# One product and one scan for two states: PSUM banks handed out in pairs, in a two-layer scan and expert network

## The chip, the cores and the metric

The kernel runs on one core of one Trainium2 chip. The metric is the device time of one execution in microseconds (us): 3631.21 us, the median of three runs of the kernel before (3628.26 to 3633.24).

## The reference, cut to what matters

The input is `x`, 8 images of 256 channels and 32x32 positions. Two layers follow each other, and each adds a mixer and then a feed-forward part to its input. Layer 0 mixes with a selective scan over the 1024 positions of an image, for 512 channels with 16 states each, and then sends each token to the two best of 8 experts. Layer 1 has depthwise convolutions, a smaller scan (64 channels, 16 states), and a feed-forward part for the 511 best-ranked tokens of an image. The part that the change touches is the scan, the same in both layers:

```
dt  = softplus(dtr @ W_dt + b_dt);  A = -exp(A_log)
dA  = exp(dt[..., None] * A)                         # per channel and state
dBu = (dt * xs)[..., None] * Bm[:, :, None, :]
h[t] = dA[t] * h[t-1] + dBu[t],  h[-1] = 0
y[t] = sum over states of h[t] * Cm[t];   y = y + xs * Dp;   y = y * silu(z)
```

## The kernel before, in words

Positions are cut into halves of N = 512. A *unit* is one half of one image; there are 16, in the order image 0 first half, image 0 second half, image 1 first half and so on. In a unit the 512 channels are four chunks of 128 partitions, taken two at a time (`cp`), and the 16 states are taken two at a time (`sp`). So a unit has 2x8x2 = 32 calls of `scan_pair`, each for one chunk and two states. Layer 1's scan (`mamba_scan`) has four groups of two images and 16 calls in each, so that there are 576 calls and 1152 states in all.

One call of `scan_pair` does the following. POOL multiplies `dtx` by the broadcast rows of B for both states at once into `dbu` (L801). Then, for each of the two states: ACT writes exp(dt*A) into a PSUM bank `h` (L806); DVE scans in place (L809), from zero in a first half and from the saved state in a second half; in a first half ACT copies the last column into `state` (L813); DVE multiplies by the row of C into `dbu` (L814). In some calls (`PAIRED`) POOL adds the two halves of `dbu` (L818). Then PE sums into `y`, in layer 0 by transposes (L793) and in layer 1 by a matmul with the identity (L828). At the end of each `cp`, DVE multiplies `y` by the gate (L875).

PSUM has eight banks of 128x512 floats. Two hold `y`. The other six are one list that two pools share: `da`, the scan states, up to three at a time, and `mm`, all other matmul outputs, up to four (five late in the program).

A planner sets the order. Every piece of work is a `step` with an engine, a cost in us, a priority (a due time), and the buffers that it reads, writes or fills. `Flow.run` takes the steps one after the other by estimated start time and emits the instructions in that order; each engine then runs its own list strictly in order, with semaphores between engines. `UNIT_AT` and `PLAN` hold the due times of units and of the later stages, and the costs in the `step` calls are figures written by hand. `warm` puts filler matmuls on `still` (L534, L538) where the planner sees PE idle. SP issues nearly all DMAs; POOL issues the indirect ones: `put` (L1129) into the experts' and tokens' slots, and gathers `ys` (L1316, L1704).

Other steps that are named below: `norm`, which POOL ends by adding a column to `xn` (L670); `delta`, which makes `dt` and `dtx` (L761 to L773); `start_turned`, in which POOL scales `xs` by the column D in two instructions (L849); `tokens`, where ACT evicts a PSUM bank (L950) and DVE takes eight more columns of the same bank (L957); the convolution taps of layer 1 on DVE (L1407); and `finish`, which ends in the last transfer.

Of the kernel before, what the change touches and what calls it, by code (L numbers as in the profile page):

```python
# [12 lines left out]
ALU = mybir.AluOpType  # L13
# [24 lines left out]
PAIRED = [3, 3, 2, 2, 0, 0, 7, 4, 4, 6, 1, 4, 0, 1, 4, 4, 4, 8, 7, 0]  # L38
# [3 lines left out]
UNIT_AT = [17, 48, 78, 109, 147, 178, 208, 241, 273, 304, 335, 368, 400, 432, 484, 518]  # L42
PLAN = [
    dict(put=7.28, experts=(179.64, 6.48), combine=(394.29, 2.87), taps=(475.51, 4.65), mamba=463.45, assemble=(516.15, 0.19), ranks=379.03, ffn=(527.6, 8.1), finish=(603.63, 3.02)),
    dict(put=10.63, experts=(348.85, 7.5), combine=(472.91, 4.35), taps=(597.89, 4.49), mamba=562.12, assemble=(556.68, 3.79), ranks=589.82, ffn=(817.97, 2.22), finish=(801.17, 11.23)),
    dict(put=5.04, experts=(457.79, 5.2), combine=(519.92, 3.42), taps=(600.24, 6.32), mamba=640.73, assemble=(726.06, 11.14), ranks=770.31, ffn=(920.6, 1.57), finish=(976.7, 8.85)),
    dict(put=5.12, experts=(583.29, 4.39), combine=(599.78, 2.06), taps=(821.99, 1.8), mamba=843.01, assemble=(797.83, 6.56), ranks=923.56, ffn=(978.1, 0.54), finish=(1005.56, 4.79)),
]

WARM = True  # L50

# [30 lines left out]
AHEAD = 100  # L82
# [33 lines left out]
class Pool:  # L116
# [4 lines left out]
    def __init__(self, make, n, in_order=True, free=None, late=None):  # L121
        self.make, self.free, self.in_order = make, [(0.0, i) for i in range(n)] if free is None else free, in_order
        self.bufs, self.queue, self.taken, self.out, self.most, self.late = [], [], 0, 0, n, late or (float("inf"), n)
        self.heir, self.got, self.handed = None, {}, 0

    def has(self, n, buf):
# [3 lines left out]
        return len(self.free) >= n and self.out + n <= most and buf.turn < self.taken + n  # L130
# [8 lines left out]
    def back(self, at, slot):  # L139

        self.out -= 1
        if self.heir is None or self.handed < len(self.bufs):
            self.free.append((at, slot))
            return
# [11 lines left out]
    def take(self, buf):  # L156
        slot = min(self.free)
        self.free.remove(slot)
# [18 lines left out]
class Flow:  # L177
# [32 lines left out]
    def run(self):  # L210
# [17 lines left out]
        def earliest(s):  # L228
# [4 lines left out]
            for b in s.fresh:  # L233
                if b.v is None:
# [3 lines left out]
                    at = max(at, sorted(b.pool.free)[k - 1][0] + HOP)  # L238
# [4 lines left out]
        def choose(e, limit):  # L243

            heap, seen, able = ready[e], [], []
            while heap and len(seen) < 40 and heap[0][0] <= limit:
# [3 lines left out]
                if at is not None:  # L250
                    switch = s.table is not None and s.table != tables[0]
                    able.append((s.prio + (4 if switch else 0), s.n, s, at, s.us + (SWITCH if switch else 0.0)))
# [3 lines left out]
            for i in able:  # L256

                if i is able[0] and i[3] <= now[e] + 0.05 or i[3] + i[4] <= able[0][3] + 0.3:
                    return i[2:]
            return able[0][2:] if able else None  # L260

        while left:
            while scans and scans[0][2].waits < 0:
                heapq.heappop(scans)
            limit = scans[0][0] + AHEAD if scans else float("inf")
# [36 lines left out]
def layers(g, ctx, x, a, out):  # L302
# [17 lines left out]
    def setup_ps():  # L320
        return g.t(g.psum, [P, N], "mm0", bufs=1)

# [33 lines left out]
    nc.vector.tensor_scalar_mul(neg_a, neg_a, -1.0)  # L356
# [90 lines left out]
    def x_tile(i):  # L447
# [3 lines left out]
    free = [(0.0, i) for i in range(6)]  # L451

# [4 lines left out]
        "mm": tiles("mm", [P, N], 4, where=g.psum, in_order=False, free=free, late=(LATE, 5)),  # L457
        "da": tiles("mm", [P, N], 3, where=g.psum, free=free),
# [87 lines left out]
    def other_weights(prio):  # L546
# [35 lines left out]
        def rest():  # L582
# [13 lines left out]
            nc.vector.tensor_scalar_mul(neg_a1, neg_a1, -1.0)  # L596
            nc.vector.tensor_scalar_mul(skip1, g.ident, ch1[:, COL_D : COL_D + 1])

        step(PE, 5.0, prio + 1, products, [loaded, w_out_t, w_xm], [t])
# [32 lines left out]
    def norm(i, prio):  # L632
# [35 lines left out]
        def shifted():  # L668
            for k in range(KC):
                nc.gpsimd.tensor_scalar(xn.v[:, k, :N], xn.v[:, k, :N], lnw[:, k, 1:2], None, ALU.add)  # L670

        gpsimd(1.2, prio + 2.2, shifted, [], [xn])

    def project(i, cp, z, prio):
# [30 lines left out]
        for n in range(2):  # L705
# [10 lines left out]
            step(ACT, 0.6, prio + n + 0.2, lambda t=t, pre=pre: nc.scalar.copy(pre.v[:, 3:], t.v), [t], fills=[pre])  # L716
# [37 lines left out]
    def delta(parts, dts, dtxs, xs, prio, soon=False):  # L754

        v, l = banks(2), buf("sq")
        for n in range(2):
            left, right, made = parts[n]
            step(PE, 0.9, prio, lambda n=n, left=left, right=right: nc.tensor.matmul(
# [13 lines left out]
        gpsimd(2.4, prio + 2, lambda: nc.gpsimd.tensor_tensor(dtxs.v, dts.v, xs.v, ALU.mult), [dts, xs], [dtxs])  # L773

    def dt_of(i, cp, prio):
# [6 lines left out]
        delta(parts, dts, dtxs, u[f"xs{cp}"], prio, soon=i == 0)  # L782
# [15 lines left out]
    def scan_pair(prio, dts, dtxs, n, bt, ct, y, scales, initial, last, stop, paired, turned=False):  # L798

        dbu = buf("dbu")  # L800
        gpsimd(2.45, prio, lambda: nc.gpsimd.tensor_tensor(  # L801
            dbu.v, dtxs.v[:, n : n + 1].to_broadcast(wide2), bt.v, ALU.mult), [dtxs, bt], [dbu], scan=True)
        for j in range(2):

            h = buf("da")
            step(ACT, 0.69, prio, lambda j=j, h=h: nc.scalar.activation(  # L806
                h.v, dts.v[:, n], AF.Exp, scale=scales(j)), [dts], [h], table="exp", scan=True)
            at = [] if initial is None else [initial[0]]
            step(DVE, 1.25, prio, lambda j=j, h=h: nc.vector.tensor_tensor_scan(  # L809
                h.v, h.v, dbu.v[:, j], 0.0 if initial is None else initial[1](j), ALU.mult, ALU.add),  # L810
                [dbu, *at], [h], scan=True)
            if last is not None:
                step(ACT, 0.19, prio, lambda j=j, h=h: nc.scalar.copy(last[1](j), h.v[:, N - 1 :]), [h], fills=[last[0]])  # L813
# [1109 lines left out]
```

## Time and profile before

| | |
|---|---|
| median of three runs | 3631.21 us |
| profiled execution: its time, its span | 3627.38 us, 3625.7 us |
| granted TensorE clock, mean | 0.936 |
| DVE, ACT, POOL busy | 2813.1, 2248.5, 2407.9 us |
| PE busy, of which filler L534 | 3075.2, 354.5 us |
| scans: first start, last start | 58.4, 3412.8 us |
| last product of a unit by its gate; end of the span | 2683, 3626 us |

The page of a profile gives busy time by engine first, and then groups of instructions: line, engine, operation, the buffers written and read, the shapes, how many; after the first bar the busy time in us and the mean of one in ns; after the second bar how long the engine had stood idle just before instructions of the group, and what ended most of that. The view of waits sums the same idle time by the instruction that waited and the one that released it: total us, times, longest. The view of stretches gives for each window its length and each engine's busy time with the number of instructions, then the granted clock, the share of the DMA engines and GB/s. In the timeline a row is its start, its length, engine, line, operation. A buffer of a scan state appears in the profile as `mm`.

### The profile page before, as it was taken

The page shows a single profiled execution, that of the slowest core. Times are in us where ns is not written, and L with a number is a line of the kernel's source. Part 1 is how long each engine was busy: PE and PEld are TensorE (multiplying, and loading weights), DVE is VectorE, ACT ScalarE, POOL GpSimd, SP SyncE. Part 2 cuts the span into 40 slices and gives each one's busy share as a digit, 9 for nine tenths or more (in the row PEclk, how much of TensorE's full clock was granted, in tenths as well). Part 3 has the DMA queues.
Part 4 walks back from the last instruction along what each step waited for, and adds up shares of the span by engine and source line. Part 5 has one row for each costly group of instructions (what it writes and reads, how often), then busy time and mean ns, then how long its engine had stood idle before and what let it go on. Part 6 is the DMA issues. An engine that isn't in the chain of part 4 may idle for free. (4 is left out here: it accounts for less than half of the span.)

```text
span 3625.7 us, 43571 instructions
## 1 busy us (share of the span) xinstructions
PE 3075.2 (85%) x13495; PEld 2061.2 (57%) x13495; DVE 2813.1 (78%) x3924; ACT 2248.5 (62%) x4241; POOL 2407.9 (66%) x1716
## 2 busy tenths in 40 slices
PE   8777878789988878978988899988888888898968
PEld 4444454545756555645655566565566665675546
DVE  4889789889877986987787989767788748858841
ACT  4466465456767656856876676766586656746533
POOL 4787678578777867996786786655686842645431
PEclk9998999899998998989999989999899988999989
DMA  6343333345745535545554568565577776886845
GB/s 234 128 132 125 119 128 127 114 139 169 247 133 191 180 133 171 184 153 177 184 184 151 169 198 267 195 201 187 171 225 254 247 243 210 296 272 218 281 150 181
DMA packets 276325, 677.00 MB, mean 187 GB/s; under 512 B 31015, under 2 KB 114861, under 8 KB 276094
## 3 DMA queue, kind: packets, MB, share of 16 engines
q1 hardware_dynamic: 257662, 623.87, 52.1%
q0 software_dynamic: 18432, 50.36, 4.4%
q8 instruction: 108, 1.77, 0.2%
q14 instruction: 123, 1.01, 0.1%
HBM read 572.92 MB, written 101.19 MB: 186 GB/s over the span
## 5 line engine op out<-in xcount | busy, mean ns | idle before, releaser
L801 POOL TENSOR_TENSOR dbu<-dtx,bc 128x1024 f32<-128x1024 f32 x556 | 1310.8, 2373 | 299.0 <-DMA bc<-rows 109.0
L809 DVE TENSOR_TENSOR_SCAN mm<-mm,dbu 128x512 f32<-128x512 f32 x570 | 697.3, 1223 | 252.5 <-ACT mm L806 195.1
L806 ACT ACTIVATE mm<-dt,neg_a 128x512 f32<-128x512 f32 x1152 | 766.6, 688 | 102.0 <-DVE dbu L814 93.8
L814 DVE TENSOR_TENSOR dbu<-mm,bc 128x512 f32<-128x512 f32 x1108 | 765.8, 691 | 50.7 <-PE y L828 0.4
L809 DVE TENSOR_TENSOR_SCAN mm<-mm,state,dbu 128x512 f32<-128x512 f32 x568 | 728.5, 1283 | 58.2 <-ACT mm L806 35.6
L793 PE MATMUL y<-ident,dbu 128*128 128x128 f32 x3628 | 533.8, 288 | 257.5 <-POOL dbu L818 122.5
L793 PEld LDWEIGHTS y<-ident,dbu 128*128 128x128 f32 x3628 | 433.4, 147 | 428.1 <-POOL dbu L818 163.1
L813 ACT COPY state<-mm 128x1 f32<-128x1 f32 x576 | 91.4, 161 | 613.8 <-DVE dbu L814 588.2
L1240 PE MATMUL mm<-we,hid 128*128 128x256 f32 x1632 | 409.4, 405 | 36.6 <-ACT hid L1224 28.9
L818 POOL TENSOR_TENSOR dbu<-dbu 128x512 f32<-128x512 f32 x214 | 278.8, 1304 | 208.2 <-DVE dbu L814 196.7
L1240 PEld LDWEIGHTS mm<-we,hid 128*128 128x128 f32 x1632 | 322.7, 203 | 118.3 <-ACT hid L1224 42.9
L1218 PE MATMUL mm<-xbt,we 128*128 128x256 f32 x1536 | 368.2, 391 | 13.5 <-ACT xbt L1206 3.5
L534 PE MATMUL y<-still 128*128 128x512 bf16 x1329 | 354.5, 406 | 0.0
L1218 PEld LDWEIGHTS mm<-xbt,we 128*128 128x128 f32 x1536 | 295.4, 196 | 79.1 <-issue 12.9
L728 PE MATMUL mm<-pre,w_tap 128*128 128x512 f32 (+3 forms) x512 | 244.2, 620 | 11.4 <-ACT pre L716 9.5
L534 PEld LDWEIGHTS <-still 128*128 128x128 bf16 x1329 | 135.8, 103 | 148.8 <-issue 51.3
L436 ACT ACT_TABLE_LOAD x169 | 216.8, 1283 | 3.0
L1704 POOL DMA_INDIRECT ys<-y,slot_t x64 | 65.4, 1021 | 214.6 <-DVE xc L1714 107.3
L1316 POOL DMA_INDIRECT ys<-slots_y,slot x128 | 128.8, 1007 | 114.1 <-DVE xo L1337 32.1
L728 PEld LDWEIGHTS mm<-pre,w_tap 128*128 128x128 f32 x512 | 95.7, 196 | 133.1 <-issue 99.9
L1224 ACT ACTIVATE hid<-mm,we 128x256 f32<-128x256 f32 x384 | 151.6, 475 | 29.1 <-PE mm L1218 25.8
L711 PE MATMUL mm<-xn,w_pre 128*128 128x512 f32 x256 | 134.5, 649 | 23.1 <-POOL xn L670 21.1
(287 smaller groups left out, 4651.2 us busy)
## 6 DMA issues: line engine op xcount, KB each, us to landing
bc<-rows SPq DMA_DIRECT2D x608, 512.0 KB
we<-in_W SPq DMA_DIRECT2D x80, 514.0 KB
we<-in_W SPq DMA_DIRECT2D x80, 512.0 KB
xb<-slots_x SPq DMA_DIRECT2D x92, 256.0 KB
slots_y<-xo SPq DMA_DIRECT2D x92, 256.0 KB
xc<-x SPq DMA_DIRECT2D x64, 256.0 KB
we<-in_W12f SPq DMA_DIRECT2D x22, 512.0 KB
slots_x<-xg SPq DMA_DIRECT2D x10, 1024.0 KB
```

What stands on the lines that cost most here:

```text
L436: nc.scalar.preload_act_table_set(tables[name])
L534: nc.tensor.matmul(live[0].v[:, 0], still, wide, start=False, stop=False)
L728: nc.tensor.matmul(tc_.v[:, cut:], w_tap[:, c, j], pre.v[:, cut + j : j + N], start=j == 3, stop=j == 0)
L793: nc.tensor.matmul(y.v[:, n, k * P : (k + 1) * P], src[:, k * P : (k + 1) * P], g.ident, start=start and k == 0, stop=stop and k == N // P ...
L801: gpsimd(2.45, prio, lambda: nc.gpsimd.tensor_tensor(dbu.v, dtxs.v[:, n : n + 1].to_broadcast(wide2), bt.v, ALU.mult), [dtxs, bt], [dbu], ...
L806: step(ACT, 0.69, prio, lambda j=j, h=h: nc.scalar.activation(h.v, dts.v[:, n], AF.Exp, scale=scales(j)), [dts], [h], table="exp", scan=True)
L809: step(DVE, 1.25, prio, lambda j=j, h=h: nc.vector.tensor_tensor_scan(h.v, h.v, dbu.v[:, j], 0.0 if initial is None else initial[1](j), AL ...
L814: step(DVE, 0.68, prio, lambda j=j, h=h: nc.vector.tensor_tensor(dbu.v[:, j], h.v, ct.v[:, j], ALU.mult), [h, ct], [dbu], scan=True)
L818: gpsimd(1.3, prio + 2.3, lambda: nc.gpsimd.tensor_tensor(dbu.v[:, 0], dbu.v[:, 0], dbu.v[:, 1], ALU.add), [], [dbu])
L1218: nc.tensor.matmul(tv[:, f], we[0].v[:, at : at + P], xbt.v[:, k], start=k == 0, stop=k == KC - 1)
L1224: nc.scalar.activation(hid.v[:, f], tv[:, f % 2], func, bias=we[0].v[:, at : at + 1])
L1240: nc.tensor.matmul(to, hid.v[:, f, h * P : (h + 1) * P], we[1].v[:, f * C : (f + 1) * C], start=extra is None and f == 0, stop=f == FC - 1,)
```

## The change

1. *Two states in two banks.* The six banks are allocated as three tiles of two. The pool `da` now hands out whole pairs (at most two), and `mm` hands out single halves, first those whose neighbour is taken. In `scan_pair` both exponentials go into one pair. In a first half one scan runs over all 1024 columns, and in both halves one product does both states, as does one copy of the last columns.
2. *From zero in the middle.* For the one scan to start anew at column 512, the decay there has to be zero. `delta` sets the first column of `dt` to 1e30 after `dtx` is made, and A is kept at or below -1e-27, so that the exponential is zero.
3. *Readers of one bank.* The state copy is made to follow the product, with a priority one later, and `raw` to follow ACT's eviction.
4. *POOL.* The shift at the end of `norm` and the scaling in `start_turned` become tensor_tensor operations with a broadcast column. `PAIRED` rises from 218 calls with the add to 316.
5. *The planner.* Costs of most steps are other figures; how much later a step may be and still go ahead of the first one in line, what a table load counts and how far other work may run ahead of the scans are now numbers in `KNOB`; `UNIT_AT` and `PLAN` have new due times.

```diff
-PAIRED = [3, 3, 2, 2, 0, 0, 7, 4, 4, 6, 1, 4, 0, 1, 4, 4, 4, 8, 7, 0]
-UNIT_AT = [17, 48, 78, 109, 147, 178, 208, 241, 273, 304, 335, 368, 400, 432, 484, 518]
+PAIRED = [4, 2, 3, 2, 0, 6, 8, 4, 8, 3, 6, 5, 7, 6, 4, 0, 7, 7, 8, 0]
+UNIT_AT = [5, 42, 75, 113, 153, 184, 214, 245, 274, 307, 340, 371, 403, 436, 484, 522]
...
-AHEAD = 100
+KNOB = [0.37, 0.11, 0.4, 0.49, 0.65, 2.04, 561.87]
...
+    def choices(self):
+        if self.pairs is None:
+            return sorted(self.free)
+        at = {slot: time for time, slot in self.free}
+        if self.pairs:
+            return sorted((max(at[k], at[k + 1]), k // 2) for k in at if k % 2 == 0 and k + 1 in at)
+        return [i[1:] for i in sorted((slot ^ 1 in at, time, slot) for time, slot in self.free)]
...
-        "mm": tiles("mm", [P, N], 4, where=g.psum, in_order=False, free=free, late=(LATE, 5)),
-        "da": tiles("mm", [P, N], 3, where=g.psum, free=free),
+        "mm": Pool(lambda i: twos[i // 2][:, i % 2], 4, in_order=False, free=free, late=(LATE, 5), pairs=False),
+        "da": Pool(lambda i: twos[i], PAIRS, free=free, pairs=True),
...
-                nc.gpsimd.tensor_scalar(xn.v[:, k, :N], xn.v[:, k, :N], lnw[:, k, 1:2], None, ALU.add)
+                nc.gpsimd.tensor_tensor(xn.v[:, k, :N], xn.v[:, k, :N], lnw[:, k, 1:2].to_broadcast([P, N]), ALU.add)
...
+        for n in heads:
+            gpsimd(0.1, prio + 2.1, lambda n=n: nc.gpsimd.memset(dts.v[:, n, :1], FAR), [], [dts])
...
+        h = buf("da")
         for j in range(2):
-            h = buf("da")
-            step(ACT, 0.69, prio, lambda j=j, h=h: nc.scalar.activation(
-                h.v, dts.v[:, n], AF.Exp, scale=scales(j)), [dts], [h], table="exp", scan=True)
-            at = [] if initial is None else [initial[0]]
-            step(DVE, 1.25, prio, lambda j=j, h=h: nc.vector.tensor_tensor_scan(
-                h.v, h.v, dbu.v[:, j], 0.0 if initial is None else initial[1](j), ALU.mult, ALU.add),
-                [dbu, *at], [h], scan=True)
-            if last is not None:
-                step(ACT, 0.19, prio, lambda j=j, h=h: nc.scalar.copy(last[1](j), h.v[:, N - 1 :]), [h], fills=[last[0]])
-            step(DVE, 0.68, prio, lambda j=j, h=h: nc.vector.tensor_tensor(
-                dbu.v[:, j], h.v, ct.v[:, j], ALU.mult), [h, ct], [dbu], scan=True)
+            step(ACT, 0.69, prio, lambda j=j: nc.scalar.activation(
+                h.v[:, j], dts.v[:, n], AF.Exp, scale=scales(j)), [dts], fills=[h], table="exp", scan=True)
+            if initial is not None:
+                step(DVE, 1.29, prio, lambda j=j: nc.vector.tensor_tensor_scan(
+                    h.v[:, j], h.v[:, j], dbu.v[:, j], initial[1](j), ALU.mult, ALU.add),
+                    [dbu, initial[0]], [h], scan=True)
+        if initial is None:
+            step(DVE, 2.32, prio, lambda: nc.vector.tensor_tensor_scan(
+                h.v.rearrange("p s n -> p (s n)"), h.v.rearrange("p s n -> p (s n)"),
+                dbu.v.rearrange("p s n -> p (s n)"), 0.0, ALU.mult, ALU.add), [dbu], [h], scan=True)
+        product = step(DVE, 1.22, prio, lambda: nc.vector.tensor_tensor(
+            dbu.v, h.v, ct.v, ALU.mult), [h, ct], [dbu], scan=True)
+        if last is not None:
+            step(ACT, 0.17, prio + 1, lambda: nc.scalar.copy(
+                last[1](), h.v[:, :, N - 1 :]), [h], fills=[last[0]]).needs.add(product)
...
-            for n in range(2):
-                c = 2 * cp + n
-                nc.gpsimd.tensor_scalar(own.v[:, n], xs.v[:, n], ch[:, c, COL_D : COL_D + 1], None, ALU.mult)
+            skips = ch[:, 2 * cp : 2 * cp + 2, COL_D : COL_D + 1]
+            nc.gpsimd.tensor_tensor(own.v, xs.v, skips.to_broadcast(wide2), ALU.mult)
...
-            step(ACT, 0.5, now + 0.5, evict, [po], fills=[xu, mv])
+            evicted = step(ACT, 0.4, now + 0.5, evict, [po], fills=[xu, mv])
             xus.append(xu)
-            step(DVE, 0.17, now + 0.5, lambda po=po, j=j: nc.vector.tensor_copy(
-                raw.v[:, j], po.v[:, P : P + E]), [po], fills=[raw])
+            step(DVE, 0.17, now + 0.7, lambda po=po, j=j: nc.vector.tensor_copy(
+                raw.v[:, j], po.v[:, P : P + E]), [po], fills=[raw]).needs.add(evicted)
```

In the file after the change the exponential is L832, the scans are L835 (from a state) and L839 (from zero), the product is L842, the copy L846, the multiply of `dbu` L827, the add L850, the scaling L880 and the transposes onto `y` L819.

## The prediction

> **What bounds the kernel now.** I read the page first, then the waits, then busy time by stretches cut where a unit's scans end, and then a few microseconds of timeline. The page:
>
> ```profile
> PE 3075.2 (85%) x13495; PEld 2061.2 (57%) x13495; DVE 2813.1 (78%) x3924; ACT 2248.5 (62%) x4241; POOL 2407.9 (66%) x1716
> ...
> L801 POOL TENSOR_TENSOR dbu<-dtx,bc 128x1024 f32<-128x1024 f32 x556 | 1310.8, 2373 | 299.0 <-DMA bc<-rows 109.0
> L809 DVE TENSOR_TENSOR_SCAN mm<-mm,dbu 128x512 f32<-128x512 f32 x570 | 697.3, 1223 | 252.5 <-ACT mm L806 195.1
> L806 ACT ACTIVATE mm<-dt,neg_a 128x512 f32<-128x512 f32 x1152 | 766.6, 688 | 102.0 <-DVE dbu L814 93.8
> L814 DVE TENSOR_TENSOR dbu<-mm,bc 128x512 f32<-128x512 f32 x1108 | 765.8, 691 | 50.7 <-PE y L828 0.4
> L809 DVE TENSOR_TENSOR_SCAN mm<-mm,state,dbu 128x512 f32<-128x512 f32 x568 | 728.5, 1283 | 58.2 <-ACT mm L806 35.6
> ...
> L813 ACT COPY state<-mm 128x1 f32<-128x1 f32 x576 | 91.4, 161 | 613.8 <-DVE dbu L814 588.2
> ...
> L818 POOL TENSOR_TENSOR dbu<-dbu 128x512 f32<-128x512 f32 x214 | 278.8, 1304 | 208.2 <-DVE dbu L814 196.7
> ```
>
> No engine is full. PE's 85% contains the filler matmuls on `still` (L534, 354.5 us), so its real work is far lower. DVE is the fullest with real work, and it stands idle in one place above all: 252.5 us before scans that start from zero, 58.2 us before scans that start from a state. Only the first kind is followed by the state copy L813, before which ACT stood 613.8 us. The waits name both:
>
> ```profile
> DVE mm L809 <- ACT mm L806: 230.7, 129, 12.1
> ACT state L813 <- DVE dbu L814: 588.2, 447, 5.7
> ```
>
> By stretches, one unit each (two second halves of a sequence, which start from a state, around a first half), and the tail after the last unit:
>
> ```profile
> core 0: us, PE busy (x) PEld busy (x) DVE busy (x) ACT busy (x) POOL busy (x), PEclk, DMA share, GB/s
> ...
> 808.00:944.00 136.00, 124.64 (x616) 87.16 (x617) 129.46 (x144) 99.42 (x159) 112.54 (x78) 0.96 0.59 196
> 944.00:1111.00 167.00, 142.43 (x620) 99.43 (x618) 116.69 (x132) 112.11 (x232) 124.85 (x77) 0.93 0.50 168
> 1111.00:1258.00 147.00, 132.70 (x615) 93.62 (x616) 129.63 (x144) 113.95 (x180) 118.31 (x72) 0.95 0.57 190
> ...
> 2683.00:3626.00 943.00, 806.49 (x3355) 563.87 (x3355) 638.08 (x1243) 524.45 (x985) 455.41 (x425) 0.94 0.72 234
> ```
>
> Second halves are bound by DVE (129.5 of 136 us); a first half has less DVE work and takes 20 to 30 us more. Summing the idle before L809 in the waits view of each unit gives 228 us in the eight first halves and 66 us in the eight second halves. The timeline of a first half shows the tie:
>
> ```profile
> 1012.22 0.69 DVE L814 TENSOR_TENSOR dbu<-mm,bc 128x512 f32<-128x512 f32 x1
> 1012.83 1.22 DVE L809 TENSOR_TENSOR_SCAN mm<-mm,dbu 128x512 f32<-128x512 f32 x1
> 1014.09 0.69 DVE L814 TENSOR_TENSOR dbu<-mm,bc 128x512 f32<-128x512 f32 x1
> ...
> 1012.95 0.16 ACT L813 COPY state<-mm 128x1 f32<-128x1 f32 x1 [1.47 <-DVE dbu L814]
> 1013.00 0.70 ACT L806 ACTIVATE mm<-dt,neg_a 128x512 f32<-128x512 f32 x1
> ```
>
> The copy could follow the scan (done 1012.19), but goes only when the product, which reads the same bank, has ended (1012.91). The exponential queued behind it is late by as much. The planner's order did not know of this wait.
>
> **The change part by part.** Sums are against the profiled execution, 3627.4 us (span 3625.7); the median of the runs is 3.8 us above it.
>
> *DVE, fewer and longer instructions.* 1152 products of 512 columns become 576 of 1024; 576 zero-start scans become 288. Length from the trace: L1622 takes 480 ns at 256 columns and 749 at 512, 1.05 ns a column, so a product of 1024 is 691+538=1229 ns and a scan, at two such steps a column, 1223+1076=2299 ns. Starts in the timeline give the cadence: a product's last 0.08 us lies beside the next instruction, so a zero-start state takes 1.87 us (1012.22 to 1014.09) and a pair 3.74; after, 2.30+0.03+1.23-0.08=3.48. A pair from a state takes 3.84 (1.92 each, at 3378.97); after, 1.28-0.08+1.28+0.03+1.23-0.08=3.66. Saved: 288x0.26+288x0.18=127, of which a few per cent lie where DVE is idle anyway: -120. The Trainium skill (Perfetto Trace Analysis, Optimizing Scalar/DVE Operations) puts the overhead of one DVE instruction on PSUM at about 125 ns: 864 instructions fewer would be 108 us, against 127. I keep the trace's.
>
> *ACT copies.* 576 copies of 161 ns become 288 of two columns (-46 us of ACT), each made to follow its product, one priority later, so that the next exponentials stand ahead of it. In the built order table loads on ACT rise by 35 of 1.28 us (+45), which cancels that; ACT is at 62%, so neither is on the path by itself. What counts is the wait: first halves have 228-66=162 us more scan idle than second halves, and copies are the difference between them. I take two thirds back, -105 (bounds 0 and -162). Late next would be POOL's `dbu` (L801) and the PSUM pair.
>
> *PSUM pairs.* Scan states had three single banks of six; now two pairs, four banks. In the built order 98 of the 576 pairs take the same two banks as the pair before them (5 of 1152 states did so before): 41 from zero, 57 from a state. There the scan waits for copy and exponentials: 0.16+2x0.69+0.15 of hand-offs=1.7 us from zero (one scan of both states needs both), 0.69+0.2=0.9 from a state. 41x1.7+57x0.9=121 us at most, 0 at least; some repeats stand where other DVE work lies between, or where the scan waited already. I take +60.
> The same section of the skill speaks against the change: where Scalar and Vector are not saturated but cause bubbles, "breaking up instructions may allow work to be completed sooner." Weighed by it, each of 288 zero-start pairs waits for one more exponential, 0.69 us: +199, and with -120 the kernel would be slower, 3706. The rows say that DVE is saturated in second halves, and in first halves ACT has 55 us free of 167 (944 to 1111), so with two pairs in turn the second exponential hides behind the scan before. I take the rows.
>
> *POOL.* `PAIRED` sends 316 pairs, not 218, through the add L818: +98x1.304=+128 us. One 1024-column multiply in place of two L849 (64x1.58 against 32x2.37) is -25, the shift at L670 (32x1.57 against about 1.30) -9, 36 memsets of 0.117 +4: +98 us of POOL. PE gets 98x4 transposes fewer. The adds wait for products, and behind them on POOL's queue stand the next L801 and indirect DMAs. Summing durations over the built order, POOL has 1111 us and DVE 1014 in units 6 to 13: POOL would lead by 98. Bounds 0 and +98; buffers of six `dbu` let it run ahead, so +30.
>
> *Moved stages.* After the last unit the built order leaves the same work: DVE 624 us (636 before), ACT 528 (531), POOL 395 (394), PE 628 (620) without fillers. So the tail of 943 us, fed by PE, DMA and chains of `ys` gathers, should stay: 0, bounds -30 and +30. SP issues as many transfers as before, the `bc` loads still in order of scans. At the start `xn` of unit 1 now stands before the first scan on DVE (58 us); a few us, within those bounds. `raw` L957 now always follows ACT's eviction, as it did at 68.1 us of its waits already: 0. Cost figures and `KNOB` alter only the order.
>
> Sum: -120-105+60+30=-135, so 3492, and with the 3.8 us of the median 3496.
>
> **Rivals.**
> - *Second pair comes late (slower).* Six banks serve pairs and up to four or five matmul outputs; a pair needs both neighbours free. The built order fixes who follows whom, so each expert or projection output evicted late by ACT holds up exponentials, and with them a scan that needs both. For it: DVE's longest wait on L806 is 12.1 us, and pairs repeat already 17% of the time. Against it: while DVE works a pair for 3.5 us, ACT needs 1.4. All pairs exposed would cost 288x(1.7+0.9)=749 us. It decides where that passes the 225 won: 30% of all pairs. At 40%: 300-225=+75, about 3700.
> - *POOL becomes the bound.* Full 98 us, and half of the copy gain: -120-50+60+98=-12, 3615.
> - *The copies still block.* They are fewer but still sit on an in-order queue. Without their gain: -120+60+30=-30, 3597. The change would not do what its ordering says.
>
> **How the numbers follow.** A difference of 0.2% is about what a measurement of this kernel can tell from none. Likeliest case 0.47, its own range 3400 to 3570. Copies still block 0.13, faster. POOL bound 0.14: 0.10 faster, 0.04 the same. Late pairs 0.26: 0.23 slower, 0.02 the same, 0.01 faster. Together 0.71, 0.06, 0.23. The range for 8 in 10 runs from 3375 (a copy gain of 130 and no pair exposed: 3627-120-130) to 3660, which holds the two small gains and part of the late pairs.
>
> **What would show it.** Right: product rows of about 1.23 us and zero-start scans of about 2.30; idle before scans in first halves under 100 us; ACT's idle before L846 well under 300; first halves of units no longer than second halves. Wrong: DVE's wait on the exponentials L832 above 230 us in total (late pairs), or POOL near full in units 6 to 13 with scans waiting for `dbu` (POOL bound). A tail longer by more than 30 us would upset the sum apart from all this.

## The result: slower, 3743.19 us

The changed kernel takes 3743.19 us (median of four runs, 3738.43 to 3751.45), the kernel before 3631.34 us in the same comparison: 1.0311 times as long, with an interval of 1.029 to 1.0333. The profiled execution took 3739.9 us, its span 3738.2 us. The prediction was 3496 us. The page after, the engines and the groups that answer to those shown of before:

```profile
PE 3082.7 (82%) x13147; PEld 2026.9 (54%) x13147; DVE 2764.0 (74%) x3060; ACT 2301.2 (62%) x3982; POOL 2471.2 (66%) x1819
...
L832 ACT ACTIVATE two<-dt,neg_a 128x512 f32<-128x512 f32 x1152 | 790.4, 690 | 152.8 <-DVE dbu L842 116.9
L835 DVE TENSOR_TENSOR_SCAN two<-two,state,dbu 128x512 f32<-128x512 f32 x564 | 726.3, 1288 | 179.7 <-ACT two L832 146.4
L839 DVE TENSOR_TENSOR_SCAN two<-two,dbu 128x1024 f32<-128x1024 f32 x284 | 650.6, 2291 | 225.1 <-ACT two L832 195.6
L842 DVE TENSOR_TENSOR dbu<-two,bc 128x1024 f32<-128x1024 f32 x552 | 675.8, 1224 | 31.3 <-DVE two L835 0.4
...
L846 ACT COPY state<-two 128x2 f32<-128x2 f32 x288 | 46.4, 161 | 264.7 <-DVE dbu L842 259.0
```

The product and the scan from zero have nearly the lengths that were predicted (1224 and 2291 ns), and ACT stands idle for 264.7 us before the copies instead of 613.8. Yet no engine is busy for a larger share of the span than before. DVE's idle time (span less busy time) grew by 162 us, from 812.6 to 974.2, and 94 of these lie before the scans: 252.5 + 58.2 us before, 225.1 + 179.7 after. The scans from a state, which in the kernel before hardly waited, now wait as long as the others, for the exponentials (waits view of after):

```profile
DVE two L839 <- ACT two L832: 195.6, 67, 23.4
DVE two L835 <- ACT two L832: 147.8, 68, 15.1
```

By stretches, a second half (1074 to 1223) and the tail after the last unit:

```profile
1074.00:1223.00 149.00, 126.69 (x573) 85.27 (x573) 121.19 (x104) 101.71 (x155) 108.56 (x70) 0.95 0.49 159
2717.00:3738.00 1021.00, 845.80 (x3458) 582.81 (x3456) 629.64 (x1157) 522.77 (x962) 439.63 (x406) 0.92 0.66 217
```

Second halves, which DVE all but filled before (129.5 of 136 us), now leave it idle: it is busy for 121 of 149 us. Three places lost time. The first scan starts at 78.1 us instead of 58.4. The scans of layer 0 take 2638.7 us from there instead of 2624.4. The tail takes 1021 us instead of 943, although only PE, whose fillers are counted too, has more to do in it: DVE is busy for 629.6 us against 638.1, ACT for 522.8 against 524.5, POOL for 439.6 against 455.4. A longer tail with no more work in it was the first sign that something other than the scans had changed.

The timeline of after shows what (ACT first, then DVE):

```profile
1007.70 0.58 ACT L1299 COPY xo<-two 128x512 f32<-128x512 f32 x1 [1.77 <-DVE xn L682]
1008.32 1.42 ACT L832 ACTIVATE two<-dt,neg_a 128x512 f32<-128x512 f32 x2
...
1006.94 1.38 DVE L682 SCALAR_TENSOR_TENSOR xn<-two,ln,sq 128x512 f32<-128x512 f32 x2
```

L1299 evicts an expert's output, L682 normalises the input of a later unit. They have no data in common, but in the built program both read the tile `two1`, each another half of it, and the one semaphore for which the eviction waits there is that of L682. The eviction waited 1.77 us, and the next two exponentials stand behind it on ACT.

### The profile page after: what moved, and what is told of

Read it like the earlier page. It is cut to its first block, busy times and chain, and to the rows that moved or that the text cites. A ratio compares the mean times of both kernels' runs of the same rounds, so it can differ in the third digit from the quotient of the medians.

```text
span 3738.2 us, 41496 instructions
## 1 busy us (share of the span) xinstructions
PE 3082.7 (82%) x13147; PEld 2026.9 (54%) x13147; DVE 2764.0 (74%) x3060; ACT 2301.2 (62%) x3982; POOL 2471.2 (66%) x1819
## 5 line engine op out<-in xcount | busy, mean ns | idle before, releaser
L827 POOL TENSOR_TENSOR dbu<-dtx,bc 128x1024 f32<-128x1024 f32 x554 | 1305.6, 2370 | 189.7 <-DMA bc<-rows 77.8
L832 ACT ACTIVATE two<-dt,neg_a 128x512 f32<-128x512 f32 x1152 | 790.4, 690 | 152.8 <-DVE dbu L842 116.9
L835 DVE TENSOR_TENSOR_SCAN two<-two,state,dbu 128x512 f32<-128x512 f32 x564 | 726.3, 1288 | 179.7 <-ACT two L832 146.4
L839 DVE TENSOR_TENSOR_SCAN two<-two,dbu 128x1024 f32<-128x1024 f32 x284 | 650.6, 2291 | 225.1 <-ACT two L832 195.6
L842 DVE TENSOR_TENSOR dbu<-two,bc 128x1024 f32<-128x1024 f32 x552 | 675.8, 1224 | 31.3 <-DVE two L835 0.4
L819 PE MATMUL y<-ident,dbu 128*128 128x128 f32 x3240 | 474.5, 289 | 206.6 <-DVE dbu L842 98.1
L819 PEld LDWEIGHTS y<-ident,dbu 128*128 128x128 f32 x3240 | 386.2, 148 | 391.1 <-POOL dbu L850 159.1
L850 POOL TENSOR_TENSOR dbu<-dbu 128x512 f32<-128x512 f32 x310 | 399.3, 1289 | 267.6 <-DVE dbu L842 261.5
L1271 PE MATMUL two<-we,hid 128*128 128x256 f32 x1600 | 401.1, 402 | 35.7 <-ACT hid L1255 8.4
L1249 PE MATMUL two<-xbt,we 128*128 128x256 f32 x1552 | 391.6, 406 | 42.4 <-ACT xbt L1237 10.5
L1249 PEld LDWEIGHTS two<-xbt,we 128*128 128x128 f32 x1552 | 308.7, 204 | 117.3 <-ACT xbt L1237 16.9
L1271 PEld LDWEIGHTS two<-we,hid 128*128 128x128 f32 x1600 | 311.2, 201 | 109.8 <-issue 14.5
L752 PE MATMUL two<-pre,w_tap 128*128 128x512 f32 (+3 forms) x512 | 235.4, 599 | 14.7 <-ACT pre L740 8.3
L1735 POOL DMA_INDIRECT ys<-y,slot_t x64 | 65.5, 1024 | 229.8 <-DVE xc L1745 98.5
L846 ACT COPY state<-two 128x2 f32<-128x2 f32 x288 | 46.4, 161 | 264.7 <-DVE dbu L842 259.0
L1255 ACT ACTIVATE hid<-two,we 128x256 f32<-128x256 f32 x388 | 152.6, 474 | 30.8 <-PE two L1249 11.1
```

Of the source, the lines that this page charges most:

```text
L752: nc.tensor.matmul(tc_.v[:, cut:], w_tap[:, c, j], pre.v[:, cut + j : j + N], start=j == 3, stop=j == 0)
L819: nc.tensor.matmul(y.v[:, n, k * P : (k + 1) * P], src[:, k * P : (k + 1) * P], g.ident, start=start and k == 0, stop=stop and k == N // P ...
L827: gpsimd(2.38, prio, lambda: nc.gpsimd.tensor_tensor(dbu.v, dtxs.v[:, n : n + 1].to_broadcast(wide2), bt.v, ALU.mult), [dtxs, bt], [dbu], ...
L832: step(ACT, 0.69, prio, lambda j=j: nc.scalar.activation(h.v[:, j], dts.v[:, n], AF.Exp, scale=scales(j)), [dts], fills=[h], table="exp", ...
L835: step(DVE, 1.29, prio, lambda j=j: nc.vector.tensor_tensor_scan(h.v[:, j], h.v[:, j], dbu.v[:, j], initial[1](j), ALU.mult, ALU.add), [db ...
L839: step(DVE, 2.32, prio, lambda: nc.vector.tensor_tensor_scan(h.v.rearrange("p s n -> p (s n)"), h.v.rearrange("p s n -> p (s n)"), dbu.v.r ...
```

## Theories and experiments

- *F, false sharing* (formed after the second run). The three tiles of the change have two banks each. The semaphores between engines are drawn by tile, not by bank. So an instruction on one half waits for other engines' instructions on the other half: two states of a pair, or two matmul outputs that have nothing to do with each other. The planner, which hands out banks, does not know of it, and neither did the prediction.
- *P, pairs starve.* A pair needs both neighbours free, so exponentials come late (the prediction's first rival).
- *Q, the new places of the stages cost time.*
- *R, any new order costs some per cent*, as places were fitted to the old one.

Each run is compared with runs of the kernel before on the same chip (3613.8 to 3619.8 us there), and ratios are to that.

**The change's new structure at the old places** (`places_old`).

```diff
-UNIT_AT = [5, 42, 75, ...], PLAN, PAIRED, KNOB of after
+UNIT_AT = [17, 48, 78, ...], PLAN, PAIRED of before; KNOB = [0.3, 0.3, 0.3, 0.3, 0.3, 4, 100]
```

> The kernel after with UNIT_AT, PLAN, PAIRED and KNOB of before (all else, the new costs too, stays). Theory P (the pairs starve: a pair that is used twice running, or was lent to a matmul, costs more than merging saves): still 3680 to 3760, scans still idle 300 us or more before units end. Theory Q (the new places are what cost: first scan at 78 us instead of 58, tail of 1021 us instead of 943): under 3620, first scan back near 58 us and tail near 943. Theory R (any new order of this planner costs 1 to 3%): somewhere between 3640 and 3800 with no pattern.

Measured 3950.45 us, 1.0923 [1.0895, 1.0951]: 207 us slower than after, and above every range that was expected. With the old places the changed kernel is slower still, so the new ones are not what it lost by: Q falls.

**Single banks at the new places** (`singles_new`): one bank, scan, copy and product for each state, the banks being halves of the same three tiles.

```diff
-"da": Pool(lambda i: twos[i], PAIRS, free=free, pairs=True)
+"da": Pool(lambda i: twos[i // 2][:, i % 2], 3, free=free, pairs=False)
```

> The kernel after with scan states in single banks again, three at most, a scan, a product and a copy for each state; new costs, places and POOL operations stay, and the copy still follows its product. Theory P: faster than after, 3600 to 3690, since the idle before scans falls although 127 us of merging are given up. Theory Q: slower than after by up to those 127 us, 3760 to 3870, since places are the same. Theory R: no pattern.

Measured 4590.59 us, 1.2671 [1.2637, 1.2704]. That is far from what was expected: without pairs the kernel became 847 us slower. The waits view has the reason, in lines that the data do not explain:

```profile
DVE dbu L838 <- ACT two L832: 162.7, 146, 5.4
...
DVE dbu L838 <- PE two L1266: 70.1, 23, 5.0
```

L838 is the product. It follows its own scan on DVE, and that scan has waited for its own exponential. So a product that waits for an exponential waits for another state's, and it has nothing at all to get from the expert matmul L1266. This run gave theory F.

**The scan part alone, on the kernel before** (`pairs_only`): pairs, merged scan, product and copy; old planner, costs, places and POOL work. **The readers' order alone** (`readers_only`): single banks of before, with

```diff
-            if last is not None:
-                step(ACT, 0.19, prio, lambda j=j, h=h: nc.scalar.copy(last[1](j), h.v[:, N - 1 :]), [h], fills=[last[0]])
-            step(DVE, 0.68, prio, ...)
+            product = step(DVE, 0.68, prio, ...)
+            if last is not None:
+                step(ACT, 0.19, prio + 1, lambda j=j, h=h: nc.scalar.copy(
+                    last[1](j), h.v[:, N - 1 :]), [h], fills=[last[0]]).needs.add(product)
```

and `raw` after ACT's eviction.

> The kernel before with the scan part of the change alone: pairs of banks, one product, one scan from zero, one copy after the product; old costs elsewhere, old places, old POOL operations. Theory P: slower than before, 3660 to 3760. Theory Q: faster by the merging, 3500 to 3600. Theory R: 3640 to 3800.

> The kernel before with its readers ordered as in the change and nothing else: each state copy follows its product with priority one later, raw follows ACT's eviction. The prediction's term for the copies (162 us more idle before scans in first halves, two thirds won back) would give 3500 to 3560. If the copy was only where ACT happened to wait and ACT's time was free, 3600 to 3660.

`pairs_only` took 4031.12 us, 1.1129 [1.11, 1.1157], again above every range that was expected; `readers_only` 3537.28 us, 0.9767 [0.9742, 0.9792], as expected from the copies. The two halves of the idea have opposite signs. The waits of `readers_only`, ACT's and DVE's:

```profile
ACT state L815 <- DVE dbu L812: 380.8, 367, 7.7
DVE mm L809 <- ACT mm L806: 129.7, 62, 6.5
```

against 588.2 and 230.7 us before. The copies still wait, but with the exponentials ahead of them.

**The test of F from both sides.** `halves_freed` is the changed kernel with the same instructions in the same order. Only waits differ: those between the halves of a tile are taken out, and each PSUM instruction waits for the last user of its own bank on every other engine, and for what it shares in SBUF. The core of it, when an instruction `ins` on `banks` is emitted and `e` is another engine:

```diff
...
+                for b in banks:
+                    last = self.users.get((b, e))
+                    if last is not None:
+                        keep[last.name] = last
+                for last in keep.values():
+                    self.tc.add_manual_dep(ins, last.name, SYNC, reason="what it touches")
+                for b in banks:
+                    if b ^ 1 not in banks and (b ^ 1, e) in self.users:
+                        self.tc.declare_no_dep(ins, group=f"bank{b ^ 1}{e}", keep=list(keep.values()), reason="another bank")
...
```

`singles_apart` is `singles_new` with six tiles of one bank; with that, a free bank is also chosen by another rule (the one that came free first, not first one whose neighbour is taken). `before_halves` is the kernel before with its six tiles made as halves of three. `control_pace` is the kernel before with `PACE = 1.06` in the planner, 1.05 before: another order, nothing else.

> The changed kernel with the same instructions in the same order on every engine; only what the instructions on PSUM wait for is different. The three tiles have two banks each. In the changed kernel an instruction on one half of a tile waits for instructions of the other engines on the other half, as if both were one place; here it waits only for those on its own bank (and for what it reads and writes in SBUF). Theory F (false sharing: the halves of a tile are serialised as one): these waits are what ate the gain; the idle time of the two kinds of scan (179.7 + 225.1 us) falls below 300 us, the wait of the 128x512 evictions for matmuls of another block goes, the first scan starts earlier than 78 us, and the time falls from 3743 to 3450-3600 us. Theory P (a pair comes late because both of its banks must be free): that is unchanged here, so the time stays within 1% of 3743 us. Theory Q (the new places of the stages cost time): unchanged too, within 1% of 3743 us.

> The kernel of singles_new (the changed kernel with one bank, one scan, one copy and one product per state, new costs, new places, new GpSimd forms) with one difference: the six banks are six tiles of one bank, as in the kernel before, instead of the halves of three tiles. Number of banks, order of the instructions and planner are the same. Theory F: the 27% of singles_new were waits between halves; the time falls from 4591 to 3500-3700 us, and the products' idle time from 606 us to under 150 us. Theory Q (the new places or costs do not fit single banks): it stays above 4300 us. Where between 3500 and 3700 it lands, against the 3537 us of readers_only, is the price of the new places, costs and GpSimd forms.

> The kernel before with one difference: its six one-bank tiles of PSUM are made as the halves of three two-bank tiles. No instruction, no order, no number of banks is changed, and nothing is merged. Theory F: waits between unrelated halves appear, and the time rises by 10 to 30%, from 3620 to 3980-4700 us, with the product waiting for the exp and for matmuls. Without false sharing: within 0.3% of the kernel before, since the addresses and the order are the same.

> The kernel before with one constant of its planner nudged (PACE 1.05 to 1.06): no stage, tile or instruction is changed, only the order in which some steps are issued. Theory R (any new order costs a per cent or more against places that were fitted to the old one): 3640-3750 us. Theories F, P and Q need nothing here: within 0.5% of the kernel before. It gives the size below which a difference between two orders is not to be read as the effect of an edit.

| kernel | us | ratio | against | difference |
|---|---|---|---|---|
| `halves_freed` | 3499.23 | 0.9674 [0.9649, 0.9699] | after, 3743.19 | -244 |
| `singles_apart` | 3472.53 | 0.9597 [0.9568, 0.9626] | `singles_new`, 4590.59 | -1118 |
| `before_halves` | 4439.65 | 1.2286 [1.225, 1.2322] | before, 3613.78 | +826 |
| `control_pace` | 3755.41 | 1.0372 [1.0327, 1.0417] | before, 3613.78 | +142 |

F is shown, by two pairs of kernels in whose built programs not one instruction stands at another place: sharing tiles makes the kernel before 23% slower (`before_halves`), and taking out the waits between halves makes the changed kernel 244 us faster (`halves_freed`). `singles_apart` is no such pair, though it was expected to be: the other choice of banks gave another order (1197 of DVE's 3924 records differ in operation or shape from the one at the same place in `singles_new`), so that its 1118 us are sharing and order together. The timeline of `before_halves`, DVE and then PE:

```profile
1107.13 1.28 DVE L807 TENSOR_TENSOR_SCAN two<-two,state,dbu 128x512 f32<-128x512 f32 x1
1111.19 0.69 DVE L812 TENSOR_TENSOR dbu<-two,bc 128x512 f32<-128x512 f32 x1 [2.77 <-PE two L1216]
...
1108.47 2.68 PE L1216 MATMUL two<-xbt,we 128*128 128x256 f32 x8 [1.92 <-DVE two L807]
```

The expert matmul waits 1.92 us for a scan on the other half of its tile (`two2`), runs 2.68 us, and the product of that scan waits 2.77 us, until the matmul is done.

In `halves_freed` the groups that stood above read:

```profile
L884 ACT ACTIVATE two<-dt,neg_a 128x512 f32<-128x512 f32 x1152 | 790.7, 690 | 175.1 <-DVE dbu L894 144.2
L887 DVE TENSOR_TENSOR_SCAN two<-two,state,dbu 128x512 f32<-128x512 f32 x564 | 726.3, 1288 | 121.1 <-ACT two L884 71.4
L891 DVE TENSOR_TENSOR_SCAN two<-two,dbu 128x1024 f32<-128x1024 f32 x284 | 650.6, 2291 | 195.9 <-ACT two L884 158.3
```

The eviction of the timeline above (L1351, as L1299 in after) waits in it only for its own matmul, and runs at the same time as the normalisation of the other half (L734):

```profile
961.47 0.59 ACT L1351 COPY xo<-two 128x512 f32<-128x512 f32 x1 [0.82 <-PE two L1323]
...
961.58 1.38 DVE L734 SCALAR_TENSOR_TENSOR xn<-two,ln,sq 128x512 f32<-128x512 f32 x2
```

The tail is back at 943 us with the same instructions as after (stretches view):

```profile
2556.00:3499.00 943.00, 810.54 (x3458) 569.19 (x3456) 629.49 (x1157) 521.17 (x963) 439.07 (x406) 0.95 0.71 235
```

So the gain lay in all three places (239 us between the two profiled executions): 78 in the tail, 153 in the scans of layer 0 (2638.7 to 2486.0 us), 8 before the first scan. The Trainium skill (PSUM — Partial Sum Buffer, "PSUM bank collisions raise a hardware error") asks for a guard by bank and quadrant of the partitions, with a guard by bank as the simple version. A guard by tile of two banks is coarser than either, and the 244 us between the medians are what it cost here beyond a guard by bank.

`control_pace` confirms R in part: one constant of the planner moves this kernel by 3.7%. A difference of a few per cent between two orders is therefore no proof that an edit caused it. The next runs repeat the main pairs under that nudge.

**Repeats under other orders, and a mixed form.** `hybrid_freed` is `halves_freed` in which only scans from zero use pairs, and scans from a state take two single banks ahead. `freed_pace`, `singles_pace` and `readers_pace` are `halves_freed`, `singles_apart` and `readers_only` with

```diff
-PACE = 1.05
+PACE = 1.06
```

> halves_freed with one edit: only the scans that start from zero (first halves and the first half of each group of layer 1) use a pair of banks, one scan and one product for two states; the scans that start from a kept state take single banks again (two of them ahead), each with its own scan of about 1288 ns and product of about 691 ns. Waits are by bank as in halves_freed. If what pairs cost lies in the state scans (there the pair waits for both exps although no scan is saved): 3440-3490 us, below halves_freed and singles_apart. If the pairs cost nothing there: about 22 us more of products (288 pairs x (2 x 691 - 1224) ns = 45 us, half hidden), so 3500-3540 us.

> halves_freed with the planner's PACE nudged from 1.05 to 1.06, nothing else: another order of the same instructions. Against halves_freed (3499 us) it shows how far one order is from another when the waits are by bank. From control_pace (3.7% above the kernel before): 3500-3650 us.

> singles_apart with PACE nudged from 1.05 to 1.06, nothing else. If the merging is worth what the prediction said (about 120 us less on VectorE, of which pairs give back some), freed_pace is faster than this one by 30 us or more, although halves_freed was 27 us slower than singles_apart; if merging and pairs cancel, the two are within the scatter of orders, some 1-2%, of each other. Expected 3480-3640 us.

> readers_only with PACE nudged from 1.05 to 1.06: to be read against control_pace (3755 us), which has the same nudge without the readers' order. If the gain of readers_only (2.3%) is the state copies that no longer hold up the exps, it is there again: 60-130 us below control_pace, 3620-3695 us. If the 2.3% was the luck of one order: anywhere from 3500 to 3800 us, with ScalarE's idle time before the copies no smaller than the 685.6 us of control_pace.

`freed_pace4` and `singles_pace4` have 1.04. `freed_unmerged` takes pairs with a scan and a product for each state (the copy stays one for both), and `pairs_only_freed` is `pairs_only` with waits by bank.

> halves_freed with pairs taken and given back as before, but with nothing merged on VectorE: each state has its own scan (about 1223 or 1288 ns) and its own product (about 691 ns). If the prediction's terms were right in size, pairing alone costs some 60 us over singles_apart (3473) and the merging takes 120 us off: 3530-3560 us here, above halves_freed (3499). If merging gains little because a merged scan waits for both exps, and the product for both scans, this one is at or below halves_freed: 3440-3500 us.

> The kernel of pairs_only (the kernel before with pairs, one product, one zero scan and one copy for two states, at the old places) with waits by bank instead of by tile. Against pairs_only (4031 us) it tells the price of the waits between halves at the old places; against readers_only (3537 us, single banks at the old places) what merging and pairs are worth there. False sharing: 3500-3650 us; if the merging pays on its own, below 3537 us.

> halves_freed with PACE 1.04 instead of 1.05: a third order of the same instructions (the others took 3499 and 3677 us). 3500-3680 us.

> singles_apart with PACE 1.04: a third order of single banks (the others took 3473 and 3485 us). 3470-3550 us. If pairs cost more than the merging gains, it is again below freed_pace4.

| order | before | readers' order, single banks | single banks, new places | pairs and merging, new places, waits by bank |
|---|---|---|---|---|
| PACE 1.05 | 3613.8 | 3537.3 | 3472.5 | 3499.2 |
| PACE 1.06 | 3755.4 | 3550.6 | 3485.2 | 3677.3 |
| PACE 1.04 | | | 3471.2 | 3697.2 |

`hybrid_freed`: 3641.09 us, 1.007 [1.0045, 1.0095]; `freed_unmerged`: 3650.12, 1.0099 [1.0081, 1.0117]; `pairs_only_freed`: 3756.24, 1.0395 [1.0369, 1.0421]. Each of these runs with pairs and waits by bank came out slower than was expected (`hybrid_freed`, `freed_pace`, `freed_unmerged`, `pairs_only_freed` and `freed_pace4`), and `readers_pace` faster; the two with single banks lay within their ranges. What follows:

- *Readers' order.* It gains 83 us in one order (against 3619.8 in its own comparison) and 205 in the other, with `raw` moved in both. ACT's waits in `control_pace` and then in `readers_pace`, copies behind the product:

```profile
ACT state L813 <- DVE dbu L814: 685.6, 487, 9.5
```

```profile
ACT state L815 <- DVE dbu L812: 373.8, 356, 7.1
```

- *New places, costs and POOL forms*, on single banks with the readers' order: 65 us faster in both orders (3537.3 to 3472.5, 3550.6 to 3485.2). They were run together and are not told apart.
- *Pairs with merging, false sharing gone:* slower than single banks in each of four comparisons, by 27, 192 and 226 us at the new places and by 219 at the old (3756.2 against 3537.3, where the single banks have `raw` moved as well). The choice of banks that goes with pairs is part of each difference. The single banks' three orders lie within 14 us of each other; the pairs' spread over 198. So P holds beside F, though not as a steady price. The 27 may in part be the waits put in by hand: two scans in a row stand 98 ns apart in `halves_freed` and 35 in after, some 260 times, which is an estimate of 16 us.
- *Pairing and merging apart*, in one order each: pairs alone cost 178 us (3472.5 to 3650.1), merging on top of them took 151 back (to 3499.2). With a spread of 198 us between orders of pairs these two sizes are rough. The mixed form was expected below 3490 if the scans from a state carried the price; it was 142 above `halves_freed`, which gives no support to that and, within the same spread, does not refute it.

The view of waits has the price of pairs on ACT: the exponentials waiting for the product, which holds the pair. First `singles_pace`, then `freed_pace`:

```profile
ACT mm L831 <- DVE dbu L837: 119.9, 117, 2.8
```

```profile
ACT two L884 <- DVE dbu L894: 203.3, 121, 6.4
```

In `freed_pace` the scans then wait longer too:

```profile
L891 DVE TENSOR_TENSOR_SCAN two<-two,dbu 128x1024 f32<-128x1024 f32 x285 | 653.1, 2292 | 301.4 <-ACT two L884 205.7
L887 DVE TENSOR_TENSOR_SCAN two<-two,state,dbu 128x512 f32<-128x512 f32 x562 | 724.0, 1288 | 175.4 <-ACT two L884 106.1
```

against 143.2 and 64.6 us in `singles_pace`.

The version that beats both kernels is `singles_apart`: 3472.53 us, 4% below the kernel before, and within 13 us of that in its two other orders. It is the change without its title: readers' order, new places, costs and POOL work, on six single banks. Its page, ACT and then DVE:

```profile
L831 ACT ACTIVATE mm<-dt,neg_a 128x512 f32<-128x512 f32 x1152 | 771.8, 688 | 125.7 <-DVE dbu L837 109.0
L834 DVE TENSOR_TENSOR_SCAN mm<-mm,dbu 128x512 f32<-128x512 f32 x570 | 696.5, 1222 | 155.3 <-ACT mm L831 78.2
L837 DVE TENSOR_TENSOR dbu<-mm,bc 128x512 f32<-128x512 f32 x1112 | 768.6, 691 | 49.3
L834 DVE TENSOR_TENSOR_SCAN mm<-mm,state,dbu 128x512 f32<-128x512 f32 x564 | 723.4, 1283 | 45.8 <-ACT mm L831 27.3
...
L840 ACT COPY state<-mm 128x1 f32<-128x1 f32 x576 | 90.1, 159 | 350.9 <-DVE dbu L837 337.6
```

## Why the prediction was wrong, step by step

- *The step that failed: "PSUM pairs", +60.* It took the built order as saying who waits for whom, and counted only pairs that repeat. The waits are drawn by tile, and the step had read of the change only that the banks are handed out by twos, not that they had become halves of shared tiles. That left out 244 us, shown by `halves_freed`.
- *The same step was too small even without that.* The built order has 73 repeated pairs, not 98: 41 from zero, as the prediction has it, and 32 from a state, not 57. In layer 0, with waits by bank, DVE stood idle before the 29 from a state for 1.70 us on average, sized at 0.9 (2.86 in after), and before the 40 from zero for 1.59, sized at 1.7 (1.74 in after). That is 113 us, near the step's upper bound of 121 and not half of it, though some scans may have waited there in any case. Over all of layer 0's scans DVE's idle time with pairs and waits by bank is 78 us larger than with single banks in one order (358 against 281), and 248 and 258 in the two others.
- *DVE, -120.* The lengths were right (1224 for 1229, 2291 for 2299 ns), but the sum of them was not. Where nothing waits, a pair from zero takes 3.52 us from start to start in after (median; 3.48 predicted, 3.74 before), and a pair from a state 3.79 (3.66 predicted, 3.85 before):

```profile
1081.65 2.61 DVE L835 TENSOR_TENSOR_SCAN two<-two,state,dbu 128x512 f32<-128x512 f32 x2
1084.30 1.23 DVE L842 TENSOR_TENSOR dbu<-two,bc 128x1024 f32<-128x1024 f32 x1
1085.44 2.61 DVE L835 TENSOR_TENSOR_SCAN two<-two,state,dbu 128x512 f32<-128x512 f32 x2
```

The working let the second of two scans start 0.08 us before the first one's end. Two scans of 1.288 us take 2.61 here: the second starts 0.035 us after it, and not one of the 263 such neighbours in after overlaps. The start that is 0.08 us early is seen behind products, and of these merging leaves half. So merging is worth some 80 us (288x0.22+288x0.06), not 127, most of it in scans from zero; the other estimate, 108, was too large as well. The time that DVE's records cover in layer 0 says the same: 71 us less with merging (2198.7 us in `singles_apart`, 2127.7 in `halves_freed`), while the sum of the records falls by 116.

- *Copies, -105.* Right in kind, and -83 and -205 in two orders. Scan idle in first halves went from 228 to 130 us in `readers_only`. In after it was 187, and that of second halves rose from 66 to 150. Table loads, set against the shorter copies, rose by 29 (355 to 384), not 35.
- *POOL, +30, and moved stages, 0.* POOL is nowhere near full (66% in after, 71% in `halves_freed` and `singles_apart`). The new places with POOL's changes and the new costs gained 65 us on single banks, where the sum had +30. The tail, given as 943, is 943 once false sharing is gone.
- *The rule that was set aside.* The prediction weighed "breaking up instructions may allow work to be completed sooner" (the Trainium skill, Perfetto Trace Analysis, Optimizing Scalar/DVE Operations) and kept the trace's sum. In each of four comparisons the single banks with broken-up instructions were faster. The reason that was weighed, 0.69 us for each pair from zero, did not show: `freed_unmerged` breaks instructions up within pairs and was not faster than merging in them (3650 against 3499, one order each). What remains is that a single bank comes free with its own product, and a pair only with the last of its two states; that fits the exponentials' waits above, but was not tried by itself.
- *Rivals.* "Second pair comes late" named the place where the wait shows (DVE on the exponentials, 343 us against its sign of 230), and its price of +75 came nearest to the measured +112. Its cause, pairs that come free late, holds in part: that is what pairs still lose to single banks with waits by bank. Late evictions that hold a neighbour were not told apart in it. The 244 us are something else, evictions, matmuls and scans waiting for banks that they never touch. The two other rivals do not explain the loss: POOL stayed at 66%, and ACT's wait before the copies fell to 264.7 us, under the 300 of the prediction's sign. The sign for the tail, over 30 us longer, did come, and rightly upset the sum.

`halves_freed` at 3499 us is no late proof of the 3496. Errors cancel there (new places that gained, merging and pairs that cost more than they saved), which is luck, and other orders of it took 3677 and 3697.

## What to carry to other kernels

Before merging buffers into one tile, find out by what unit the waits are drawn: an order that is free by bank can be serial by tile, and the sign is an instruction that waits for an engine from which it gets nothing. When two small buffers become one, the gain in instructions must be held against buffers that come free only together. And before a few per cent are put down to an edit, nudge a constant of the planner once: here that alone moved the kernel by 3.7%.

## What was not expected of the machine

- The sum of an engine's records is not the time that it covers, and not every record overlaps the next. Behind a product the next DVE instruction started some 80 ns before the record's end (786 times before scans in the layer 0 of the kernel before). Behind a scan that another scan followed it never did: 0 of 263 in after.
- The granted TensorE clock was 0.880 in `singles_new` and 0.889 in `before_halves`, the two runs with the most waiting, against 0.936 before and after and 0.943 in `halves_freed`. What lowers it was not tested.
